# Four PSUM tiles of two banks, and one row maximum and one exponential for two heads

## The chip, the cores and the metric

The kernel runs on one core of a Trainium2 chip. The metric is the time of one execution on the device, in microseconds (us). The core has a matrix engine (TensorE, PE in the profile; its weight loads are listed apart as PEld), a vector engine (VectorE, DVE), a scalar engine (ScalarE, ACT), GpSimd (POOL) and a queue engine that issues most transfers (SyncE, SP). Matrix products land in PSUM, which has eight banks; one bank holds 512 fp32 numbers in each of 128 partitions. DVE and ACT read PSUM and so make its banks free again.

## The reference

Eight batches of 512 rows of 128 channels go through four layers. Each layer has an attention part and a feed-forward part, and each part is added to x after a layer norm: `x = x + layernorm(part(layernorm(x)))`. The two parts that the change edits directly are the softmax attentions of the first and of the fourth layer, with 16 heads of 8 channels:

```python
# layer 0 (and layer 3, there with a rotary embedding and a division by sqrt(8))
scores = jnp.einsum('hbqd,hbkd->hbqk', Q, K)
atten = jax.nn.softmax(scores, axis=-1)
out = jnp.einsum('hbqk,hbkd->hbqd', atten, V).reshape(b, s, -1)
```

Between them lie a gated mixer, a learned recurrence, a top-1 routed expert layer with a capacity, a linear attention and a top-k expert layer; after them four dense experts with weights for each row. All of it is fp32.

## The kernel before

It runs in three stages, told apart by what the engines do: stage I (about 0 to 740 us of the profiled execution) is the attention of layer 0, with the mixer, the recurrence and the routing as background work; stage II (about 740 to 1340 us) holds the rest of layers 0 and 1 and layer 2, many short chains taken in turns; stage III (about 1340 us to the end) is the attention of layer 3 with the dense experts as background work.

Instructions stand on each engine in the order in which the program writes them (`tc.manual_schedule()`); every engine works through its own list in order and waits at an instruction until the semaphores of that instruction allow it. The waits are put in by the framework, from the tiles that an instruction reads and writes.

**Attention.** A call is one batch with four heads; there are 32 calls in each attention. `Attention.run` goes through steps `g`, four steps (128 query rows each) to a call, so 128 steps in each attention. A step does two things for different calls. `score` takes the step `g + 7`: for each of four heads a product of queries with keys (tile `at_s`, L393), 128 rows by 512 columns in one bank, and on DVE the negated row maximum (`at_mx`, L394). `weigh` takes the step `g`: for each of four heads the transposed product (`at_st`, L400) with the row maximum already in it as an extra channel, and on ACT the exponential (`at_e`, L403). The four heads lie in four groups of 32 partitions (`32 * h`). A step writes these in the order score 0, weigh 2, score 1, weigh 3, then some background (`bg.between()`), then score 2, weigh 0, score 3, weigh 1, then the rest of the background (`bg.pull`). The four products of a half step thus use all four row groups of the matrix engine.

Once in four steps `maxima` turns the row maxima by a matrix transpose (`at_mx_ps`, L372), copies them on ACT (`at_mt`, L374) and sends them by four transfers on SP into the operand of `weigh`; `total_up` adds up the weighted values (`at_o`, 16 products, L411) with a copy on ACT (`at_ot`, L419); `finish` transposes that (`at_ops`, L425), and DVE divides (L428, L429).

**Background.** Generators that yield costs of PE and DVE. In stage III the largest is `L3Ffn.body`: `hidden` is one product (`l3f_h_ps`, L1923) with a relu on ACT (`l3f_hT`, L1924), `result` is four products (`l3f_y_ps`, L1930) with a weighted addition on DVE (`l3f_o`, L1933). `flip` (L239, copy on ACT L240) is a transpose of four blocks used everywhere.

**PSUM.** All eight banks are one ring: `bank()` hands out the next of eight tiles of one bank each. A new tile waits until the tile that had the bank eight requests earlier has been read. Scores and background draw from the same ring: a step takes eight banks for scores, and the background takes 1045 banks over the whole program.

Of the kernel before, what the change touches and what calls it, by code (L numbers as in the profile page):

```python
# [9 lines left out]
F32 = mybir.dt.float32  # L10
I32 = mybir.dt.int32
AF = mybir.ActivationFunctionType
ALU = mybir.AluOpType
AX = mybir.AxisListType
# [3 lines left out]
P = 128  # L18
# [3 lines left out]
NJ = S // P  # L22
# [48 lines left out]
class Ctx:  # L71


    def __init__(self, es: ExitStack, tc: tile.TileContext, consts: bass.AP):
        self.tc = tc
        nc = self.nc = tc.nc
        pool = lambda name, bufs, **kw: es.enter_context(tc.tile_pool(name=name, bufs=bufs, **kw))
        self.keep = pool("keep", 1)
        self.shared = pool("shared", 2)
        self.dram = pool("dram", 1, space=DRAM)  # L80

        self.c = self.keep.tile([P, C_ALL], F32, name="consts_sb", tag="consts_sb")
        nc.sync.dma_start(self.c, consts)
        self.ident = self.c[:, C_ID : C_ID + P]
        self.triu = self.c[:, C_TRIU : C_TRIU + P]
        self.ones = self.keep.tile([P, P], F32, name="ones", tag="ones")
        nc.vector.memset(self.ones, 1.0)
        self.mhalf = self.keep.tile([P, 8], F32, name="mhalf", tag="mhalf")
        nc.vector.memset(self.mhalf, -0.5)
        self.x = [self.keep.tile([P, NJ, D], F32, name=f"x{b}", tag=f"x{b}") for b in range(B)]  # L90

        self.home = self.keep

        self.ps = pool("ps", 1, space=PSUM)
        self.turn = [0]
        es.enter_context(tc.manual_schedule())

        self.brisk = False

    RING = 8  # L100

    @contextmanager
    def phase(self, name):
# [7 lines left out]
    def beside(self, name, side="left"):  # L111

        other = copy(self)
        with self.tc.tile_pool(name=name, bufs=2, side=side) as other.w:
            other.home = other.w
            yield other

    def bank(self, name):
        self.turn[0] += 1
        return self.ps.tile([P, 512], F32, name=name, tag=f"bank{self.turn[0] % self.RING}", bufs=1)  # L120

    def work(self, shape, name, bufs=2, dtype=F32):
        return self.w.tile(shape, dtype, name=name, tag=name, bufs=bufs)
# [197 lines left out]
class Attention:  # L321
# [58 lines left out]
    def run(self, n_calls, load, dst, done, scale, bg):  # L380


        cx, nc = self.cx, self.cx.nc
        total = NJ * n_calls
        mx, es, ots = {}, {}, {}

        def score(g, h):
            n, c = divmod(g, NJ)
            qk = self.qks[n % self.NQK][32 * h : 32 * h + 32]
            if n not in mx:  # L390
                mx[n] = cx.work([P, NJ, 4], "at_mx", bufs=3)
            s = cx.bank("at_s")
            nc.tensor.matmul(s, qk[:, 0, c * P : (c + 1) * P], qk[:, 1, :], start=True, stop=True)  # L393
            nc.vector.tensor_reduce(mx[n][:, c, h : h + 1], s, AX.X, ALU.max, negate=True)  # L394

        def weigh(g, h):
            n, c = divmod(g, NJ)
            qk = self.qks[n % self.NQK][32 * h : 32 * h + 32]
            s = cx.bank("at_st")
            nc.tensor.matmul(s, qk[:, 1, c * P : (c + 1) * P], qk[:, 0, :], start=True, stop=True)  # L400
            if g not in es:
                es[g] = cx.work([P, 4, S], "at_e", bufs=5)
            nc.scalar.activation(es[g][:, h, :], s, AF.Exp, scale=scale)  # L403

        def total_up(n):
            o = cx.bank("at_o")
            vp = self.pads[n % self.NPAD]
            for c in range(NJ):
                e = es.pop(NJ * n + c)
                for h in range(4):  # L410
                    nc.tensor.matmul(  # L411
                        o[32 * h : 32 * h + 32, :],
                        vp[:, c, h, :],
                        e[:, h, :],
                        start=(c == 0),
                        stop=(c == NJ - 1),
                    )
            ots[n] = cx.work([P, S], "at_ot")
            nc.scalar.copy(ots[n], o)  # L419

        def finish(n):
            ot = ots.pop(n)
            t = cx.bank("at_ops")
            for c in range(NJ):
                nc.tensor.transpose(t[:, c * P : (c + 1) * P], ot[:, c * P : (c + 1) * P], cx.ident)  # L425
            t = t.rearrange("p (c h d) -> p c h d", c=NJ, h=4)
            rec = cx.work([P, NJ, 4, 1], "at_rec")
            nc.vector.reciprocal(rec, t[:, :, :, 8:9])  # L428
            nc.vector.tensor_mul(dst(n), t[:, :, :, 0:8], rec.to_broadcast([P, NJ, 4, 8]))  # L429
            done(n)  # L430

        for g in range(-self.LEAD - self.LOAD, total + 2):
            ahead = g + self.LEAD
            is_s, is_t = 0 <= ahead < total, 0 <= g < total
            n, c = divmod(ahead + self.LOAD, NJ)
            if c == 0 and 0 <= n < n_calls:
                self.fill(n, *load(n))
            for i in (0, 2):

                for h in range(2):  # L440
                    if is_s:
                        score(ahead, i + h)
                    if is_t:
                        weigh(g, 2 - i + h)
                if i == 0 and (is_s or is_t):
                    bg.between()
            spent = 0.0
            n, c = divmod(ahead - 4, NJ)
            if c == 0 and 0 <= n < n_calls:
                self.maxima(n, mx.pop(n))  # L450
            n, c = divmod(g - NJ, NJ)
            if c == 0 and 0 <= n < n_calls:
                total_up(n)
                spent += 3.6
            if c == 1 and 0 <= n < n_calls:
                finish(n)
                spent += 0.5
            if is_s or is_t:
                bg.pull(spent)
# [147 lines left out]
class Mix:  # L607
# [16 lines left out]
    def load(self):  # L624
        cx, nc = self.cx, self.cx.nc
        W_r, W_k, W_v, mu_r, mu_k = self.args
        self.mu = cx.const([D, 2], "mu")
        nc.sync.dma_start(self.mu[:, 0:1], mu_r.rearrange("(d o) -> d o", o=1))
        nc.sync.dma_start(self.mu[:, 1:2], mu_k.rearrange("(d o) -> d o", o=1))
        raws = []  # L630
        for i, w in enumerate((W_r, W_k, W_v)):
            raws.append(cx.work([P, D], f"l0f_raw{i}", bufs=1))
            nc.sync.dma_start(raws[-1], w)
        self.nu = cx.const([D, 2], "nu")
        yield
        yield
        yield
        nc.vector.tensor_scalar(self.nu, self.mu, -1.0, 1.0, ALU.mult, ALU.add)
        t = cx.bank("l0f_w_ps")
        for i in range(3):  # L640
            nc.tensor.transpose(t[:, i * P : (i + 1) * P], raws[i], cx.ident)
        w = cx.const([P, 3, P], "w0f")
        nc.scalar.copy(w[:, 0:2, :].rearrange("p i d -> p (i d)"), t[:, : 2 * P])

        nc.scalar.mul(w[:, 2, :], t[:, 2 * P : 3 * P], 0.5)
        self.wr, self.wk, self.wv = (w[:, i, :] for i in range(3))
        yield 0.4
# [1414 lines left out]
```

## Time and profile before

| | |
|---|---|
| time, three runs | 2126.2, 2128.79 (median), 2131.81 us |
| the profiled execution | 2132.52 us; its span from first to last instruction 2130.7 us |
| granted PE clock, mean of the span | 0.871 |
| busy: PEld, ACT, POOL | 1012.4, 1085.9, 500.2 us |
| L393 MATMUL at_s | 2048 records, two for each product, mean 655 ns |
| L394 TENSOR_REDUCE at_mx | 1024, mean 681 ns |
| L403 ACTIVATE at_e | 1024, mean 597 ns |
| L419 COPY at_ot | 64, mean 585 ns |
| L374 COPY at_mt | 64, mean 238 ns |
| L1924 ACTIVATE l3f_hT | 128, mean 683 ns |
| L1933 SCALAR_TENSOR_TENSOR l3f_o | 128, mean 348 ns |

Busy time of a matrix product is modelled at its end, and products in different row groups overlap, so a busy PE is not a full PE. The duration of a DVE or ACT instruction is longer than the distance to the next one behind it, because the end of one overlaps the start of the next.

### The profile page before, as it was taken

The page shows a single profiled execution, that of the slowest core. Times are in us where ns is not written, and L with a number is a line of the kernel's source. Part 1 is how long each engine was busy: PE and PEld are TensorE (multiplying, and loading weights), DVE is VectorE, ACT ScalarE, POOL GpSimd, SP SyncE. Part 2 cuts the span into 40 slices and gives each one's busy share as a digit, 9 for nine tenths or more (in the row PEclk, how much of TensorE's full clock was granted, in tenths as well). Part 3 has the DMA queues.
Part 4 walks back from the last instruction along what each step waited for, and adds up shares of the span by engine and source line. Part 5 has one row for each costly group of instructions (what it writes and reads, how often), then busy time and mean ns, then how long its engine had stood idle before and what let it go on. Part 6 is the DMA issues. An engine that isn't in the chain of part 4 may idle for free.

```text
span 2130.7 us, 31833 instructions
## 1 busy us (share of the span) xinstructions
PE 1772.0 (83%) x10886; PEld 1012.4 (48%) x10886; DVE 1290.8 (61%) x4012; ACT 1085.9 (51%) x2272; POOL 500.2 (23%) x566
## 2 busy tenths in 40 slices
PE   3999999898989967649446773799999999999996
PEld 1444545454534456437335552444554454545454
DVE  2777786777777665546447422777666666665522
ACT  1566655555554732346552221366666565665653
POOL 1001111112121122442523485222212121110001
PEclk7999988899988887659565786799999999999998
DMA  5212101011100032016214132111101010100000
GB/s 127 39 33 39 34 16 38 14 39 22 32 16 15 14 104 83 23 27 180 79 50 124 24 42 36 31 32 29 27 9 31 11 27 12 29 12 6 9 6 10
DMA packets 198064, 81.83 MB, mean 38 GB/s; under 512 B 97604, under 2 KB 189674, under 8 KB 197904
## 3 DMA queue, kind: packets, MB, share of 16 engines
q1 hardware_dynamic: 190224, 73.61, 14.3%
q0 software_dynamic: 7680, 6.19, 1.9%
q8 instruction: 87, 1.43, 0.3%
q14 instruction: 73, 0.60, 0.1%
HBM read 45.25 MB, written 31.59 MB: 36 GB/s over the span
## 4 chain that ended last, share of the span: by engine, by line
PE 55%; DVE 23%; ACT 6%; issue 6%; POOL 5%; DMA 3%; SPq 2%; POOLq 0%; ACTq 0%; DVEq 0%
PE at_o L411 11%; PE at_s L393 11%; DVE at_mx L394 8%; PE at_st L400 6%; PE l3f_y_ps L1930 5%; PE l3f_h_ps L1923 5%; DVE ln_st L203 2%; PE flip L239 2%; POOL l2f_out L1686 2%; POOL ln_rs L194 1%; PE l1f_h_ps L1155 1%; PE l1f_y_ps L1177 1%; POOL l2f_xg L1081 1%; PE at_ops L425 1%; DVE ln_mv L205 1%
## 5 line engine op out<-in xcount | busy, mean ns | idle before, releaser
L394 DVE TENSOR_REDUCE at_mx<-at_s 128x1 f32<-128x512 f32 x1024 | 642.3, 681 | 302.3 <-PE at_st L400 233.9
L393 PE MATMUL at_s<-qk 32*128 32x512 f32 x2048 | 612.0, 655 | 35.6 <-DMA qk<-qk_zero 21.3
L403 ACT ACTIVATE at_e<-at_st 128x512 f32<-128x512 f32 x1024 | 535.7, 597 | 193.6 <-PE at_st L400 152.4
L400 PE MATMUL at_st<-qk 32*128 32x512 f32 x2048 | 610.2, 655 | 18.4 <-DVE at_mx L394 12.6
L194 POOL TENSOR_TENSOR ln_rs<-ln_ve,mhalf 128x4 f32<-128x4 f32 x136 | 138.3, 1017 | 837.5 <-DVE ln_ve L188 773.7
L393 PEld LDWEIGHTS at_s<-qk 32*128 32x128 f32 x2048 | 232.2, 194 | 177.4 <-issue 57.7
L400 PEld LDWEIGHTS at_st<-qk 32*128 32x128 f32 x2048 | 240.5, 192 | 111.7 <-issue 41.8
L411 PE MATMUL at_o<-at_e,pad_v 128*32 128x512 f32 x2048 | 254.2, 641 | 14.8 <-DVE at_mx L394 14.8
L411 PEld LDWEIGHTS at_o<-at_e,pad_v 128*32 128x32 f32 x2048 | 66.9, 117 | 197.5 <-issue 173.8
L1930 PEld LDWEIGHTS l3f_y_ps<-w3f,l3f_hT 128*128 128x128 f32 x1024 | 131.8, 197 | 46.3 <-issue 26.8
L1930 PE MATMUL l3f_y_ps<-w3f,l3f_hT 128*128 128x128 f32 x1024 | 136.9, 282 | 3.2 <-ACT l3f_hT L1924 2.0
L419 ACT COPY at_ot<-at_o 128x512 f32<-128x512 f32 x64 | 37.5, 585 | 199.5 <-PE at_o L411 199.5
L1923 PE MATMUL l3f_h_ps<-l3f_xT,w3f 128*128 128x512 f32 x256 | 131.2, 611 | 0.0
L1924 ACT ACTIVATE l3f_hT<-l3f_h_ps,w3f_b1c 128x512 f32<-128x512 f32 x128 | 85.0, 683 | 64.1 <-PE l3f_h_ps L1923 64.0
L1933 DVE SCALAR_TENSOR_TENSOR l3f_o<-l3f_y_ps,l3f_w,l3f_o 128x128 f32<-128x128 f32 x128 | 44.4, 348 | 93.3 <-PE l3f_y_ps L1930 93.1
L217 ACT ACTIVATE l_xn<-x,ln_off,ln_rs 128x128 f32<-128x128 f32 x96 | 39.5, 482 | 81.5 <-DVE ln_off L211 75.4
L239 PE MATMUL flip<-consts_sb,l_xn 128*128 128x128 f32 x96 | 29.6, 398 | 54.4 <-ACT l_xn L217 54.1
L203 DVE BATCH_NORM_STATS2 ln_st<-x 128x6 f32<-128x128 f32 x256 | 55.2, 278 | 18.2 <-POOL x L937 12.4
L1686 POOL DMA_INDIRECT l2f_out<-l2f_y,l2f_idx x32 | 50.5, 1579 | 21.9 <-DVE l2f_y L1683 13.1
L1923 PEld LDWEIGHTS l3f_h_ps<-l3f_xT,w3f 128*128 128x128 f32 x256 | 42.2, 194 | 23.9 <-issue 10.0
L1773 POOL TENSOR_TENSOR l_qk<-l_r,consts_sb 128x256 f32<-128x256 f32 x32 | 21.9, 686 | 133.2 <-DVE l_r L1768 133.2
L366 POOL COPY pad_v<-l_in 128x128 f32<-128x128 f32 x32 | 9.4, 294 | 185.4 <-DMA l_in<-l_v 147.9
(412 smaller groups left out, 2551.0 us busy)
## 6 DMA issues: line engine op xcount, KB each, us to landing
l1f_w<-in_L_ffn_w SPq DMA_DIRECT2D x32, 256.0 KB
l2f_parts<-l2f_out SPq DMA_DIRECT2D x32, 256.0 KB
l2f_out<-l1f_zero SPq DMA_DIRECT2D x24, 256.0 KB
l_qk<-l_qkT SPq DMA_DIRECT2D x16, 256.0 KB
qk<-l_qk SPq DMA_DIRECT2D x128, 32.0 KB
qk<-at_mt SPq DMA_DIRECT2D x256, 2.0 KB
qk<-l_qkT SPq DMA_DIRECT2D x128, 32.0 KB
l2f_x<-l2f_rows SPq DMA_DIRECT2D x8, 272.0 KB
```

Source lines behind the costliest of these rows:

```text
L194: self.nc.gpsimd.tensor_tensor(rs, ve, self.mhalf[:, :NJ], ALU.pow)
L203: nc.vector.bn_stats(st[:, j, :], src[:, j, :])
L239: self.nc.tensor.transpose(t[:, j * P : (j + 1) * P], src[:, j, :], self.ident)
L393: nc.tensor.matmul(s, qk[:, 0, c * P : (c + 1) * P], qk[:, 1, :], start=True, stop=True)
L394: nc.vector.tensor_reduce(mx[n][:, c, h : h + 1], s, AX.X, ALU.max, negate=True)
L400: nc.tensor.matmul(s, qk[:, 1, c * P : (c + 1) * P], qk[:, 0, :], start=True, stop=True)
L403: nc.scalar.activation(es[g][:, h, :], s, AF.Exp, scale=scale)
L411: nc.tensor.matmul(o[32 * h : 32 * h + 32, :], vp[:, c, h, :], e[:, h, :], start=(c == 0), stop=(c == NJ - 1),)
L1686: nc.gpsimd.indirect_dma_start(out=self.pairs.summed[s], out_offset=bass.IndirectOffsetOnAxis(ap=idx[e][:, s : s + 1], axis=0), in_=ys[e][ ...
L1923: nc.tensor.matmul(hp, self.w1[:, e, f * P : (f + 1) * P], xt, start=True, stop=True)
L1924: nc.scalar.activation(hts[e][:, f], hp, AF.Relu, bias=self.b1c[:, f, e : e + 1])
L1930: nc.tensor.matmul(yp[:, :D], hts[e][:, f, js], self.w2[:, e, f, :], start=(f == 0), stop=(f == NF - 1))
```

## The change

PSUM becomes a ring of four tiles of two banks. `twin()` hands out a whole tile; `bank()` hands out its first half and, at the next request, its second half; a `twin()` in between drops a half that is left over. A half step of attention now asks for one tile for two `weigh` products and one for two `score` products, writes the two transposed products, then the two products for the maxima, then one exponential over 2 x 512 columns and one reduction over 2 x 512 columns. Everything else that used a bank, so all of the background, `maxima`, `total_up` and `finish`, draws halves.

```diff
         self.turn = [0]
+        self.half = []
...
-    RING = 8
+    RING = 4
...
+    def twin(self, name):
+
+        self.half.clear()
+        self.turn[0] += 1
+        return self.ps.tile([P, 2, 512], F32, name=name, tag=f"twin{self.turn[0] % self.RING}", bufs=1)
+
     def bank(self, name):
-        self.turn[0] += 1
-        return self.ps.tile([P, 512], F32, name=name, tag=f"bank{self.turn[0] % self.RING}", bufs=1)
+
+        if self.half:
+            return self.half.pop()
+        t = self.twin(name)
+        self.half.append(t[:, 1, :])
+        return t[:, 0, :]
...
-        def score(g, h):
+        def products(s, g, i, side):
+
             n, c = divmod(g, NJ)
-            qk = self.qks[n % self.NQK][32 * h : 32 * h + 32]
+            for h in (i, i + 1):
+                qk = self.qks[n % self.NQK][32 * h : 32 * h + 32]
+                nc.tensor.matmul(
+                    s[:, h - i, :],
+                    qk[:, side, c * P : (c + 1) * P],
+                    qk[:, 1 - side, :],
+                    start=True,
+                    stop=True,
+                )
+
+        def score(g, i, s):
+            n, c = divmod(g, NJ)
             if n not in mx:
                 mx[n] = cx.work([P, NJ, 4], "at_mx", bufs=3)
-            s = cx.bank("at_s")
-            nc.tensor.matmul(s, qk[:, 0, c * P : (c + 1) * P], qk[:, 1, :], start=True, stop=True)
-            nc.vector.tensor_reduce(mx[n][:, c, h : h + 1], s, AX.X, ALU.max, negate=True)
-
-        def weigh(g, h):
-            n, c = divmod(g, NJ)
-            qk = self.qks[n % self.NQK][32 * h : 32 * h + 32]
-            s = cx.bank("at_st")
-            nc.tensor.matmul(s, qk[:, 1, c * P : (c + 1) * P], qk[:, 0, :], start=True, stop=True)
+            nc.vector.tensor_reduce(mx[n][:, c, i : i + 2], s, AX.X, ALU.max, negate=True)
+
+        def weigh(g, i, s):
             if g not in es:
                 es[g] = cx.work([P, 4, S], "at_e", bufs=5)
-            nc.scalar.activation(es[g][:, h, :], s, AF.Exp, scale=scale)
+            nc.scalar.activation(es[g][:, i : i + 2, :], s, AF.Exp, scale=scale)
...
-                for h in range(2):
-                    if is_s:
-                        score(ahead, i + h)
-                    if is_t:
-                        weigh(g, 2 - i + h)
+                if is_t:
+                    st = cx.twin("at_st")
+                    products(st, g, 2 - i, 1)
+                if is_s:
+                    s = cx.twin("at_s")
+                    products(s, ahead, i, 0)
+                if is_t:
+                    weigh(g, 2 - i, st)
+                if is_s:
+                    score(ahead, i, s)
                 if i == 0 and (is_s or is_t):
                     bg.between()
```

## The prediction

> **What bounds the kernel now.** I read first the page's busy times and its slices, then the costliest groups, then busy times by stretch, then the timeline of single steps.
>
> ```profile
> PE 1772.0 (83%) x10886; PEld 1012.4 (48%) x10886; DVE 1290.8 (61%) x4012; ACT 1085.9 (51%) x2272; POOL 500.2 (23%) x566
> ...
> PE   3999999898989967649446773799999999999996
> ...
> L394 DVE TENSOR_REDUCE at_mx<-at_s 128x1 f32<-128x512 f32 x1024 | 642.3, 681 | 302.3 <-PE at_st L400 233.9
> L403 ACT ACTIVATE at_e<-at_st 128x512 f32<-128x512 f32 x1024 | 535.7, 597 | 193.6 <-PE at_st L400 152.4
> L400 PE MATMUL at_st<-qk 32*128 32x512 f32 x2048 | 610.2, 655 | 18.4 <-DVE at_mx L394 12.6
> ```
>
> PE is nearly always busy in both attention stages (slices 2 to 14 and 27 to 39), and DVE and ACT mostly wait for PE: 302.3 us ahead of the maxima, 193.6 us ahead of the exponentials, against 18.4 us of PE ahead of L400. So PE sets the pace, and the next rows show how purely:
>
> ```profile
> 300.00:400.00 100.00, 93.20 (x569) 47.79 (x563) 74.92 (x218) 56.55 (x122) 15.79 (x19) 0.83 0.14 28
> 1100.00:1200.00 100.00, 61.41 (x261) 51.26 (x260) 61.06 (x287) 25.27 (x69) 36.31 (x50) 0.53 0.30 86
> 1500.00:1600.00 100.00, 96.31 (x660) 51.12 (x660) 67.71 (x176) 61.65 (x125) 19.36 (x24) 0.98 0.09 19
> ```
>
> (After the stretch: PE, PEld, DVE, ACT, POOL busy, then the granted PE clock.) In the timeline a step's eight score products take 1.93 us when nothing holds them (1553.09 to 1555.02). Adding up the blocks of score products in the trace gives 398 us in stage I and 318 us in stage III, against 128 x 1.93 = 247 us each. So stage I has 151 us and stage III only 71 us in which score products wait or run at half clock. In stage III PE is the limit; in stage I PE and DVE (75%) hold each other up; in stage II short chains do.
>
> **Part 1: one instruction for two heads.** A back-to-back run without background shows the price of single instructions:
>
> ```profile
> 132.49 6.99 ACT L403 ACTIVATE at_e<-at_st 128x512 f32<-128x512 f32 x12 [0.35 <-PE at_st L400]
> 132.76 7.25 DVE L394 TENSOR_REDUCE at_mx<-at_s 128x1 f32<-128x512 f32 x12
> ```
>
> That is 0.604 us for a reduction and 0.583 us for an exponential (four in 2.06 us, 0.515 each, where they don't wait). No row has a pair. Statistics on DVE take 691 ns for 512 columns (L565) and 278 for 128 (L203): 1.08 ns a column, so about 0.05 us of 0.604 is fixed. ACT copies take 585 ns for 512 columns and 474 for 384: 0.87 ns a column, leaving 0.07 of 0.515. With 512 pairs each, 26 us of DVE and 36 us of ACT go away, at most 62 us if both were on the path, and nothing where PE is. The reader may also start later, but four products run side by side and both heads are ready together (products from 1559.40, first reduction at 1560.56). So start is no loss, but release is coarser: a tile is refilled only when both heads are read, 1.16 us of products after a pair of about 1.16 + 0.08 us. The round is 2.40 us, and the single heads needed 4 x 0.604 = 2.42 us a step: the saving on DVE is spent again even where DVE was the limit. I put part 1 at -25 us (bounds -62 and 0).
>
> The Trainium skill has a rule against this part. "Perfetto Trace Analysis", section "Optimizing Scalar/DVE Operations", has larger operations help where the engine is saturated, and smaller ones where it is not but makes others wait. Here DVE is 61% and ACT 51% busy, the second case; by the rule part 1 would gain nothing, and the sum below would end 25 us higher.
>
> **Part 2: the order of the products.** Score, weigh, score, weigh becomes weigh, weigh, score, score. Heads 2, 3 and 0, 1 still fill all four row groups, so 1.93 us stays. A weigh that waits now holds both score products behind it on PE; that is within the bounds of part 1.
>
> **Part 3: two banks under one tile.** This decides. The waits that the framework put into the changed program are known before it runs. Of the 1045 banks that are not scores, 453 are second halves; 448 of them have a first product that waits on its own semaphore for the instruction that *reads the first half*, though the banks differ. Before, these products had a bank of their own and waited only for a reading eight banks back. PE works in order, so everything behind stands still too: the next scores, and for those DVE and ACT. One step of stage III shows it:
>
> ```profile
> 1555.02 0.28 PE L372 MATMUL at_mx_ps<-consts_sb,at_mx 128*16 128x128 f32 x1
> 1555.14 0.60 PE L425 MATMUL at_ops<-consts_sb,at_ot 128*128 128x128 f32 x4
> 1555.60 0.66 PE L239 MATMUL flip<-consts_sb,l3f_xn 128*128 128x128 f32 x4
> 1556.09 1.02 PE L1923 MATMUL l3f_h_ps<-l3f_xT,w3f 128*128 128x512 f32 x2
> 1556.28 0.24 ACT L374 COPY at_mt<-at_mx_ps 16x128 f32<-16x128 f32 x1
> 1556.42 0.57 ACT L240 COPY l3f_xT<-flip 128x512 f32<-128x512 f32 x1
> 1557.45 1.16 PE L1930 MATMUL l3f_y_ps<-w3f,l3f_hT 128*128 128x128 f32 x8 [0.34 <-DVE at_mx L394]
> 1558.45 1.02 PE L1923 MATMUL l3f_h_ps<-l3f_xT,w3f 128*128 128x512 f32 x2
> 1558.65 0.35 DVE L1933 SCALAR_TENSOR_TENSOR l3f_o<-l3f_y_ps,l3f_w,l3f_o 128x128 f32<-128x128 f32 x1 [0.16 <-PE l3f_y_ps L1930]
> ```
>
> at_ops starts 0.12 us after at_mx_ps. As its second half it must wait for the copy at_mt, which stands behind exponentials and ends at 1556.52: 1.38 us late. The product h after flip would wait for the copy that ends at 1556.99, 0.90 us late; the product h after y for the addition that ends at 1559.00, 0.55 us late.
>
> I took this lateness for every pair in the trace of before: end of the last reader of the first half, plus 0.05 us (from a reader's end to a waiting product: an exponential ends at about 304.39, weights load at 304.43), minus the start of the second half's first product. 424 pairs could be matched by name:
>
> - stage I: 82 pairs, 112 us. Of these, at_ops behind at_mx_ps is 30 pairs at 1.93 us = 58 us.
> - stage II: 153 pairs, 166 us.
> - stage III: 189 pairs, 262 us. at_ops behind at_mx_ps 30 x 1.95 = 59, y behind h 25 x 2.20 = 55, h behind y 39 x 0.97 = 38, h behind h 11 x 1.90 = 21, the other 84 together 89.
>
> The 29 left I price at stage II's mean, 1.08 us: 32 us. All of it would be 112 + 166 + 262 + 32 = 572 us.
>
> It won't all be paid. A late reader is partly late because DVE and ACT have a backlog, and they work it off while PE waits. In stage III what remains is the reader itself: at_ops about 1.35 (the last exponential pair, about 1.0, plus 0.24 and two handovers), y behind h 0.9 (relu 0.69 and handovers), h behind y 0.6, others about 0.9. That is 41 + 23 + 23 + 10 + 76 = 173 us, 66%; I take 0.7, 183 us, since the 71 us of slack there are small. In stage I, DVE and ACT lose their feed after such a stop (in the step at 130 us, PE would resume 0.9 us later and DVE run dry), but scores that already waited for DVE hide a part: 0.6, 67 us. In stage II other chains wait anyway while PE does: 0.5 of 198, 99 us. Bounds: 0.3, 0.25 and 0.5 give 34 + 50 + 131 = 215 us; the full lateness gives 572.
>
> **Part 4: the clock of PE.** It follows PE's load in the rows above: 0.98 at 96% busy, 0.83 at 93% and 0.53 at 61%. With 183 us of stops stage III falls below 80% busy. If the clock there went from 0.98 to 0.88, some 650 us of PE work would take 72 us more, and in stage I 0.90 to 0.85 would add 33 us; half of it hides under the stops. With some 8 us in stage II I take 60 us; bounds 0 and 150.
>
> "TensorE: Matmul & The Clock Gate", section "What's actually happening", has the clock halve after an idle window of about 3.4 us. The stops here are shorter, so by the letter of that rule part 4 would be 0 and the sum 60 us lower; but the clock was 0.83 between 300 and 400 us with no gap on PE over 2.1 us. The row decides.
>
> **The sum.** 67 + 99 + 183 + 60 - 25 = 384 us. The span of 2130.7 us becomes 2515, the profiled run's 2132.5 us 2517; on the median 2128.8 it is 2513 us. The bounds added up: 215 + 0 - 62 = +153 us and 572 + 150 - 0 = +722 us. Both ends at once are unlikely; I go from 2290 to 2720.
>
> **Rivals.**
> - *The stops hide under waits that exist already.* For it: DVE and ACT wait a lot, and stage I has 151 us of slack. Against it: in stage III 71 us of slack stand against 262 us of lateness. With the low bounds 2129 + 153 to 165 = about 2285 us, chance 0.11.
> - *The clock goes down for good.* For it: 0.53 at 61% load. Full lateness and a stage III at 0.75 give 2129 + 572 + 100 = 2800 us, chance 0.12.
> - *Faster: the second half's reader is done in time.* If PE reached a second half only after the reader of the first, part 3 is nothing and part 1 counts: 2129 - 25 to - 62, about 2090 us. It decides once mean lateness falls below 25 / 453 = 0.06 us, against 540 / 424 = 1.27 us in the trace. Chance 0.03.
> - *The waits bite only in a few places and cancel with part 1*: within 0.3% (6 us, about what a measurement of this kernel can tell), 0.01.
>
> The forecast itself has 0.73: in all 0.96 slower, 0.01 same, 0.03 faster.
>
> **What would show it.** In the profile after: at_mx and at_e 512 times, at about 1.2 and 1.05 us each; at_ops beginning after the end of the copy at_mt in nearly every call; PE idle ahead of at_ops, l3f_h_ps and l3f_y_ps with ACT and DVE as releasers, some 300 us more idle PE; more half-clock time in stage III. It is wrong if stage III takes less than 100 us more, if PE does not wait before second halves, or if most of the loss stands ahead of score products.

## The result, and the profile after

The kernel after takes 2634.58 us (median of six runs, 2623.7 to 2638.7); the kernel before, run beside it on the same chip, takes 2129.82 us (median of six, 2123.37 to 2133.85). The ratio is 1.2369, with an interval of 1.2339 to 1.2399: 505 us slower, where the prediction had 384. The execution profiled took 2633.47 us, with a span of 2631.7 us and a mean granted PE clock of 0.843 against 0.871.

First the page's busy times, PE's slices, the slices of PE's granted clock, and the groups that answer to those shown of before:

```profile
PE 1897.4 (72%) x10886; PEld 1019.1 (39%) x10886; DVE 1264.0 (48%) x3500; ACT 1069.9 (41%) x1760; POOL 500.6 (19%) x566
...
PE   4888878778787666565556747877777777777776
...
PEclk9899988897988675586555866999899999999998
...
L415 DVE TENSOR_REDUCE at_mx<-at_s 128x2 f32<-128x1024 f32 x512 | 611.1, 1219 | 423.4 <-PE at_s L403 417.0
L420 ACT ACTIVATE at_e<-at_st 128x1024 f32<-128x1024 f32 x512 | 505.0, 1019 | 328.0 <-PE at_s L403 264.0
L403 PE MATMUL at_st<-qk 32*128 32x512 f32 x2048 | 578.0, 682 | 28.5 <-DVE at_mx L415 15.4
L442 PE MATMUL at_mx_ps<-consts_sb,at_ot 128*128 128x128 f32 x240 | 43.0, 306 | 89.4 <-ACT at_mt L385 89.4
```

The granted clock of the kernel before, in 40 slices of its own span, was this:

```profile
PEclk7999988899988887659565786799999999999998
```

PE was at 9 in most slices of the attention stages and is now at 7 or 8. DVE and ACT did their part of the change: 512 reductions and 512 exponentials of two heads each, 27 and 16 us less busy. Nothing else has become the limit, because DVE and ACT wait longer for PE than before (423.4 and 328.0 us ahead of these two groups, against 302.3 and 193.6). PE itself stands still. The last row names the largest single place: the transposes of `finish`, called `at_ops` before. A second half carries the name of the tile that it lies in, so here they are called `at_mx_ps`, with `finish`'s line L442. PE stood for 89.4 us ahead of them, all of it for the copy `at_mt`, which reads the other half. In the kernel before PE's waits ahead of `at_ops` were these two, 9.8 us, and none was for `at_mt`:

```profile
PE at_ops L425 <- ACT at_e L403: 8.4, 7, 2.1
PE at_ops L425 <- ACT at_ot L419: 1.4, 2, 0.7
```

PE's waits of the kernel after (releaser, us in all, times, longest) list the same thing for other pairs. L1945 is the product of `hidden` and L1952 that of `result`:

```profile
PE at_mx_ps L442 <- ACT at_mt L385: 89.4, 60, 4.2
PE l3f_y_ps L1945 <- DVE l3f_o L1955: 31.0, 39, 2.0
PE l3f_h_ps L1952 <- ACT l3f_hT L1946: 30.2, 25, 2.5
...
PE at_st L403 <- DVE at_mx L415: 15.4, 13, 2.2
```

Each of the first three lines is a product that waits for the instruction that reads the other bank of its tile. The fourth, a score product that waits for a reduction, is small and was 12.6 us before.

One stretch of the timeline in stage III, 18 us long, lets this be watched (start, length, engine and line; in brackets the idle time ahead and what ended it):

```profile
1904.90 1.02 ACT L420 ACTIVATE at_e<-at_st 128x1024 f32<-128x1024 f32 x1
1905.05 0.91 PE L1788 MATMUL l_qkv_ps<-w3a,xnT 128*128 128x384 f32 x2 [0.31 <-ACT at_e L420]
1906.58 0.28 DVE L1791 TENSOR_TENSOR l_v<-l_qkv_ps,w3a_b 128x128 f32<-128x128 f32 x1
1906.91 1.13 PE L1945 MATMUL l_qkv_ps<-l3f_xT,w3f 128*128 128x512 f32 x2 [0.95 <-DVE l_v L1791]
...
1914.93 0.59 ACT L436 COPY at_ot<-at_o 128x512 f32<-128x512 f32 x1 [2.58 <-PE at_o L428]
1915.57 0.91 PE L1788 MATMUL at_o<-w3a,xnT 128*128 128x384 f32 x2 [0.70 <-ACT at_ot L436]
...
1919.47 0.24 ACT L385 COPY at_mt<-at_mx_ps 16x128 f32<-16x128 f32 x1
1919.76 0.66 PE L442 MATMUL at_mx_ps<-consts_sb,at_ot 128*128 128x128 f32 x4 [0.76 <-ACT at_mt L385]
```

Three times a product starts 0.05 us after another engine has finished with the *other* half: 1906.58 + 0.28 = 1906.86 and the product at 1906.91; 1914.93 + 0.59 = 1915.52 and 1915.57; 1919.47 + 0.24 = 1919.71 and 1919.76. PE lost 0.95, 0.70 and 0.76 us there. The releaser named in the brackets is that reader each time.

Where the time lies, by stage. Stage I ends with the last `at_st` of the first attention, stage III begins with the first `at_s` of the second. PE's idle time is where no product ran; "lost to half clock" is half of the time in which a product ran while the granted clock was 0.5. The clock records of the traces hold two values alone, 1 and 0.5; a fall is a stretch at 0.5. Differences are taken before rounding.

| | stage I | stage II | stage III |
|---|---|---|---|
| length before, after, us | 743, 848 (+105) | 595, 738 (+143) | 792, 1045 (+253) |
| PE idle before, after, us | 89, 192 (+103) | 218, 293 (+76) | 52, 249 (+197) |
| lost to half clock before, after, us | 59, 86 (+27) | 100, 153 (+52) | 22, 51 (+29) |
| mean granted clock before, after | 0.904, 0.887 | 0.704, 0.652 | 0.965, 0.943 |
| falls to half clock before, after | 22, 36 | 23, 24 | 8, 21 |
| mean length of a fall before, after, us | 6.5, 5.3 | 15.6, 21.6 | 6.4, 5.6 |

One more sum over the traces goes to the cause: PE's idle time right ahead of the first products of the 453 second halves (before, the same products, in a bank of their own) went from 124 to 504 us, +380: 83 of it in stage I, 118 in stage II and 179 in stage III. With the 108 us of the clock (27 + 52 + 29) that is 488 of 505.

### The profile page after: what moved, and what is told of

The parts are those of the page before. It is cut to its first block, busy times and chain, and to the rows that moved or that the text cites. A ratio compares the mean times of both kernels' runs of the same rounds, so it can differ in the third digit from the quotient of the medians.

```text
span 2631.7 us, 30977 instructions
## 1 busy us (share of the span) xinstructions
PE 1897.4 (72%) x10886; PEld 1019.1 (39%) x10886; DVE 1264.0 (48%) x3500; ACT 1069.9 (41%) x1760; POOL 500.6 (19%) x566
## 4 chain that ended last, share of the span: by engine, by line
PE 52%; DVE 21%; ACT 16%; issue 5%; POOL 3%; DMA 2%; SPq 1%; ACTq 0%; POOLq 0%; DVEq 0%
PE at_st L403 9%; PE at_o L428 8%; DVE at_mx L415 7%; ACT at_e L420 6%; PE at_s L403 4%; PE l3f_y_ps L1952 3%; PE l3f_h_ps L1945 2%; DVE ln_st L214 2%; PE l3f_y_ps L1945 2%; PE at_mx_ps L442 1%; PE l1f_h_ps L1177 1%; PE l3f_h_ps L1952 1%; ACT l3f_hT L1946 1%; PE l2f_h_ps L1687 1%; ACT at_ot L436 1%
## 5 line engine op out<-in xcount | busy, mean ns | idle before, releaser
L415 DVE TENSOR_REDUCE at_mx<-at_s 128x2 f32<-128x1024 f32 x512 | 611.1, 1219 | 423.4 <-PE at_s L403 417.0
L420 ACT ACTIVATE at_e<-at_st 128x1024 f32<-128x1024 f32 x512 | 505.0, 1019 | 328.0 <-PE at_s L403 264.0
L403 PE MATMUL at_s<-qk 32*128 32x512 f32 x2048 | 577.1, 696 | 24.1 <-DMA qk<-qk_zero 21.1
L403 PEld LDWEIGHTS at_st<-qk 32*128 32x128 f32 x2048 | 190.2, 203 | 194.0 <-issue 82.7
L403 PEld LDWEIGHTS at_s<-qk 32*128 32x128 f32 x2048 | 186.5, 205 | 108.0 <-issue 54.5
L1952 PEld LDWEIGHTS l3f_y_ps<-w3f,l3f_hT 128*128 128x128 f32 x712 | 97.0, 204 | 37.8 <-issue 23.9
L442 PE MATMUL at_mx_ps<-consts_sb,at_ot 128*128 128x128 f32 x240 | 43.0, 306 | 89.4 <-ACT at_mt L385 89.4
L1952 PE MATMUL l3f_y_ps<-w3f,l3f_hT 128*128 128x128 f32 x712 | 101.6, 290 | 5.9 <-DVE l3f_o L1955 4.0
L1945 PE MATMUL l3f_h_ps<-l3f_xT,w3f 128*128 128x512 f32 x130 | 79.6, 709 | 12.2 <-ACT l3f_hT L1946 9.8
L1946 ACT ACTIVATE l3f_hT<-l3f_h_ps,w3f_b1c 128x512 f32<-128x512 f32 x65 | 44.5, 685 | 79.3 <-PE l3f_h_ps L1945 79.3
L1945 PE MATMUL l3f_y_ps<-l3f_xT,w3f 128*128 128x512 f32 x78 | 44.0, 646 | 31.0 <-DVE l3f_o L1955 31.0
L442 PEld LDWEIGHTS at_mx_ps<-consts_sb,at_ot 128*128 128x128 f32 x240 | 27.3, 150 | 100.9 <-ACT at_mt L385 100.9
```

Source lines behind the costliest of these rows:

```text
L403: nc.tensor.matmul(s[:, h - i, :], qk[:, side, c * P : (c + 1) * P], qk[:, 1 - side, :], start=True, stop=True,)
L415: nc.vector.tensor_reduce(mx[n][:, c, i : i + 2], s, AX.X, ALU.max, negate=True)
L420: nc.scalar.activation(es[g][:, i : i + 2, :], s, AF.Exp, scale=scale)
L1945: nc.tensor.matmul(hp, self.w1[:, e, f * P : (f + 1) * P], xt, start=True, stop=True)
L1946: nc.scalar.activation(hts[e][:, f], hp, AF.Relu, bias=self.b1c[:, f, e : e + 1])
L1952: nc.tensor.matmul(yp[:, :D], hts[e][:, f, js], self.w2[:, e, f, :], start=(f == 0), stop=(f == NF - 1))
```

## The experiments

Three theories stood against each other. A: the framework makes the second half's products wait for the reader of the first half. R: a ring of four coarse tiles is what hurts, whoever waits for whom inside a tile. P: the pair instructions and the order of the products hurt. All times are medians; ratios are to the kernel before on the same chip, with 95% intervals.

**Banks apart.** The kernel after, with the waits between different halves of a tile taken out wherever the two instructions share nothing else. The halves are different banks, and a bank is still waited for.

```diff
+def apart(tc, twins):
...
+    for name, us in uses.items():
+        if name.startswith(("at_s_", "at_st_")):
+            continue
+        for k, (late, h) in enumerate(us):
+            for early, g in us[:k]:
+                if h != g and late.engine != early.engine and not shares(late, early, name):
+                    tc.declare_no_dep(late, early, reason="other bank")
```

> The changed kernel with the same four tiles, order and pair instructions, but the framework is told that an access to one bank of a tile does not depend on an access to the other bank, unless the two also share another tile. The second halves' waits for the first half's reader are gone (448 before, 22 left where a real value is handed on). Theory A (the tied halves are the loss): 2090 to 2180 us, PE idle ahead of at_ops and of the expert products back to about what it was. Rival R (a ring of four coarse tiles is the loss): still over 2450 us. Rival P (pair instructions or the order of products are the loss): still over 2450 us.

2163.91 us, ratio 1.017 (1.0129 to 1.021). Of the 505 us, 471 are gone. The page shows PE back at 8 and 9 in the attention stages, with the same pair instructions:

```profile
PE 1742.7 (81%) x10886; PEld 973.5 (45%) x10886; DVE 1260.8 (58%) x3500; ACT 1059.8 (49%) x1760; POOL 500.3 (23%) x566
...
PE   3898988898888868658447783898989899999996
...
L418 DVE TENSOR_REDUCE at_mx<-at_s 128x2 f32<-128x1024 f32 x512 | 611.4, 1218 | 349.9 <-PE at_s L406 343.8
```

PE's idle time ahead of the second halves is 116 us, less than before the change. So A holds, and R and P together come to 34 us net in this form.

**The waits alone.** The kernel before, with eight tiles of one bank and single heads, and only the waits added: the first product of what would be a second half waits for the last readers of what would be its first half.

```diff
+        if name in ("at_s", "at_st"):
+            self.half.clear()
+        elif self.half:
+            self.pairs.append((self.half.pop(), t.tensor.name))
+        else:
+            self.half.append(t.tensor.name)
...
+    for first, second in pairs:
+        for r in {r.engine: r for r in reads[first]}.values():
+            tc.add_manual_dep(writes[second][0], r.name, info, reason="first half read")
```

> The kernel before with eight single banks, one head to an instruction and the old order; the only addition is that the second of each two background banks, paired as the changed kernel pairs them, waits with its first product for the last readers of the first. Theory A: 2560 to 2690 us, all of the loss without any of the change's other parts. Rivals R and P: 2130 to 2200 us.

2660.88 us, ratio 1.2507 (1.2469 to 1.2545). The whole loss appears with nothing of the change but its waits. It is even 26 us more than after; the kernel after has the pair instructions on top, and the next experiment prices them. PE's waits of this kernel name the same products and releasers:

```profile
PE at_ops L434 <- ACT at_mt L383: 118.3, 60, 4.3
PE l3f_h_ps L1932 <- DVE l3f_o L1942: 33.9, 39, 2.2
PE l3f_y_ps L1939 <- ACT l3f_hT L1933: 32.9, 25, 3.0
```

**One head at a time.** The kernel after, with each pair instruction split into two.

```diff
-            nc.vector.tensor_reduce(mx[n][:, c, i : i + 2], s, AX.X, ALU.max, negate=True)
+            for h in range(2):
+                nc.vector.tensor_reduce(mx[n][:, c, i + h : i + h + 1], s[:, h, :], AX.X, ALU.max, negate=True)
...
-            nc.scalar.activation(es[g][:, i : i + 2, :], s, AF.Exp, scale=scale)
+            for h in range(2):
+                nc.scalar.activation(es[g][:, i + h, :], s[:, h, :], AF.Exp, scale=scale)
```

> The changed kernel with its tiles and order, but each pair instruction split into two for one head each. Theory A: 2635 to 2680 us, as slow as the changed kernel or a little slower, since at most 62 us of DVE and ACT work come back. Rival P (the long instructions delay what waits for them): 2130 to 2450 us.

2689.34 us, ratio 1.2637 (1.2591 to 1.2682): 55 us more than after, and 9 us above the window of theory A, which had allowed at most 45 us for the split. The pair instructions are no part of the loss; they save. (Against the waits alone this kernel has the new order and the coarse ring too, and is 28 us slower.)

**A whole tile for every request.** The kernel after, without second halves, so that nothing can be tied; each single request uses up a tile of two banks.

```diff
         t = self.twin(name)
-        self.half.append(t[:, 1, :])
         return t[:, 0, :]
```

> The changed kernel, but bank() takes a whole new tile each time and leaves its second half unused: no tied halves, and 2069 tiles through the ring in place of 1616. Theory A: well below the changed kernel, 2200 to 2450 us, the rest being the shorter ring. Rival R (the coarse ring is the loss): above 2635 us, since the ring is used up faster still.

2239.35 us, ratio 1.0527 (1.0494 to 1.056). Throwing away every second bank of the background, which makes 2069 tiles out of 1616, costs far less than using it under the framework's waits.

**The order alone.** The kernel before, with the two transposed products and their exponentials ahead of the two others.

```diff
                 for h in range(2):
-                    if is_s:
-                        score(ahead, i + h)
                     if is_t:
                         weigh(g, 2 - i + h)
+                for h in range(2):
+                    if is_s:
+                        score(ahead, i + h)
```

> The kernel before with eight single banks and single-head instructions; only the order within a half step is new: weigh, weigh, score, score. With the banks kept apart the changed kernel was 34 us over the kernel before, though the sum had it 25 us under. If the order makes these 34 us: 2160 to 2190 us. If it is neutral, as the sum had it: 2115 to 2145 us.

2131.47 us, ratio 1.0009 (0.999 to 1.0029): no change.

**Banks apart, one head at a time.** The edits of the first and the third experiment together; their diffs are above.

> The changed kernel with the banks kept apart (2164 us) and each pair instruction split into two. If the pair instructions save and the coarse ring of four tiles costs: slower than 2164, 2185 to 2225 us. If the pair instructions themselves are what costs 34 us (a longer reader ahead of whatever takes its tile next): 2120 to 2150 us.

2189.61 us, ratio 1.0273 (1.0238 to 1.0308). Against banks apart with pairs (2163.91) the pairs save 26 us here (22 by the two ratios). What is left of the change in this kernel is the ring of four tiles and the order, and it costs some 60 us against the kernel before (0.0273 x 2128 = 58). The order is worth nothing in the ring of eight, so the 58 us are put down to the coarse ring, as this kernel asks for its tiles.

**Banks apart, order of before.** The first experiment with the products interleaved as before, and with the tile for the maxima asked for first.

```diff
+                if is_s:
+                    s = cx.twin("at_s")
                 if is_t:
                     st = cx.twin("at_st")
-                    products(st, g, 2 - i, 1)
-                if is_s:
-                    s = cx.twin("at_s")
-                    products(s, ahead, i, 0)
+                for k in range(2):
+                    if is_s:
+                        product(s, ahead, i, 0, k)
+                    if is_t:
+                        product(st, g, 2 - i, 1, k)
```

> The changed kernel with the banks kept apart and the four products of a half step in the old order: score, weigh, score, weigh, into two tiles. If the order makes the 34 us: 2120 to 2140 us. If the coarse ring does: 2150 to 2180 us.

2205.0 us, ratio 1.0358 (1.0323 to 1.0393). A miss: neither window holds it, and it changed two things at once. The last two experiments take them apart.

**A single kind of wait.** The second experiment with only the 60 waits of `at_ops` for the copy `at_mt`.

```diff
     for first, second in pairs:
+        if not first.startswith("at_mx_ps"):
+            continue
         for r in {r.engine: r for r in reads[first]}.values():
```

> The kernel before with only 60 of the 453 waits added: at_ops waits for the copy of at_mx_ps. The lateness of these 60 pairs in the trace of before adds up to 117 us. If each stop is paid by itself, nearly in full, as the idle time ahead of at_ops in the kernel with all waits says (118 us): 2220 to 2270 us. By the factors of the prediction (0.6 to 0.7, no clock): about 2205 us. If stops hurt only in mass, through the clock: under 2170 us.

2239.82 us, ratio 1.0519 (1.0491 to 1.0546): +112 us, 1.87 us for each wait. The lateness that the prediction had read for these pairs was 58 + 59 = 117 us, so it was paid nearly whole. The 112 us hold a loss of clock too: PE's idle time grew by 102 us in all, and the loss to half clock by 32. PE stands ahead of these products:

```profile
PE at_ops L434 <- ACT at_mt L383: 116.9, 60, 4.3
```

**Leftover halves kept.** Of the coarse ring's price it was open whether it comes from the halves that are dropped when the scores ask for a tile. Here they are kept until the ring comes round.

```diff
     def twin(self, name):
-
-        self.half.clear()
...
         if self.half:
-            return self.half.pop()
+            at, second = self.half.pop()
+            if self.turn[0] - at < self.RING:
+                return second
         t = self.twin(name)
-        self.half.append(t[:, 1, :])
+        self.half.append((self.turn[0], t[:, 1, :]))
```

> As e1_banks_apart (2163.91 us), but a second half that is left over when the scores ask for a tile is kept for the next single request instead of being dropped, unless the ring has come round. Open is why e1 and e6_apart_one_head stand some 35 and 60 us above the kernel before. Theory D (the dropped halves make the ring short): 2125 to 2145 us, and PE's waits for exponentials ahead of at_mx_ps, at_o and flip, some 72 us together in e1, fall by half or more. Theory C (a tile of two banks comes free only when both heads are read, whatever the singles do): 2150 to 2175 us, with the same waits as in e1.

2160.8 us, ratio 1.017 (1.0147 to 1.0193), the same as banks apart; PE's waits for `at_e` come to 99 us in all against 96 there. The dropped halves cost nothing.

**The order of the tiles, and the order of the products.** Banks apart with one of the two changes each: first only the tile for the maxima asked for ahead of the other, as shown, then only the interleaved products, as in the diff of banks apart, order of before.

```diff
+                if is_s:
+                    s = cx.twin("at_s")
                 if is_t:
                     st = cx.twin("at_st")
                     products(st, g, 2 - i, 1)
                 if is_s:
-                    s = cx.twin("at_s")
                     products(s, ahead, i, 0)
```

> As e1_banks_apart, products in the same order (two transposed ones first), but the tile for the maxima is asked for ahead of the tile for the exponentials. e7_apart_old_order changed this and the order of the products together and took 2205.0 us, 41 more than e1. Theory T (the order of the tiles counts: the first single bank after a half step then comes back from a reduction of about 1.2 us in place of an exponential of about 1.0 us): 2195 to 2215 us, PE's waits ahead of at_mx_ps and at_o are for at_mx. Theory O (the order of the products counts): 2155 to 2175 us.

> As e1_banks_apart, tiles asked for in the same order, but the products interleaved as in the kernel before (maxima, transposed, maxima, transposed). Theory T: 2155 to 2175 us. Theory O: 2195 to 2215 us, since each of the two tiles is complete only after the last pair of products.

2205.39 us, ratio 1.0389 (1.0346 to 1.0432), for the tiles; 2171.48 us, ratio 1.0234 (1.0201 to 1.0267), for the products. So it is the order in which tiles are asked for. That the tile asked for first is also the one filled last is not the reason: banks apart, order of before (2205.0 us, ratio 1.0358) and the second kernel here (2171.48, 1.0234) fill both tiles side by side and differ in the order of asking alone. PE's waits, of banks apart and then with the tile for the maxima first, show what it changes:

```profile
PE at_mx_ps L386 <- ACT at_e L423: 24.8, 49, 2.7
PE at_st L406 <- ACT at_e L423: 21.6, 18, 2.0
PE at_o L431 <- ACT at_e L423: 10.7, 28, 0.9
```

```profile
PE at_st L406 <- DVE at_mx L418: 45.7, 39, 3.9
PE at_mx_ps L386 <- DVE at_mx L418: 34.2, 60, 1.3
PE at_o L431 <- DVE at_mx L418: 28.2, 45, 1.5
```

The same products wait, but for the reduction in place of the exponential. The first background tile after a step takes over the tile that the step asked for first; it comes free when both heads in it are read. The reduction takes 1.22 us and the exponential 1.02, and the waits for either come to 114 us in banks apart (96 for `at_e`, 18 for `at_mx`) and to 179 us with the other order (24 and 155). In the kernel before they were 59 us (15 and 44), and with banks apart and one head at a time 129 (106 and 24). So the coarse ring adds 55 to 70 us of such waits, about its price of 58.

## Why the prediction was right, and where it was off

**Part 3 was the cause, and right in size.** The prediction summed the lateness of the first halves' readers, took part of it, and got 349 us of stops; PE's idle time ahead of second halves grew by 380. By stage it planned 67, 99 and 183 us. Ahead of the second halves PE's idle time grew by 83, 118 and 179: 0.74, 0.60 and 0.68 of the lateness, where 0.6, 0.5 and 0.7 had been taken. PE's whole idle time grew by 103, 76 and 197, so in stage II some 42 us of the new stops only took the place of old ones, as the prediction argued. The weak step is the backlog that ACT and DVE were to work off while PE stands, so that of `at_ops` only 1.35 of 1.95 us would remain. With these 60 waits alone there was no such relief: PE stood 116.9 us ahead of `at_ops`, 1.95 each, and with all waits 118.3. In the kernel after it is 89.4, 1.49 each, but there the `at_mx_ps` ahead of it waits 24.9 us for exponentials. For h behind y 31.0 of 39 x 0.97 = 38 us were paid, and for y behind h 30.2 of 55, where the prediction kept 23 us for either.

**Part 4 was mis-sized, and put in the wrong place.** The sum had 60 us for the clock; the loss to half clock grew by 108 us. The prediction expected stage III to fall from 0.98 to 0.88 when it is less than 80% busy. It fell from 0.965 to 0.943 over the whole stage. These are the three stretches of the kernel after that answer to those shown of before (PE, PEld, DVE, ACT, POOL busy, then the granted clock):

```profile
300.00:400.00 100.00, 78.61 (x472) 35.37 (x471) 62.40 (x175) 47.41 (x77) 17.71 (x20) 0.82 0.12 25
1100.00:1200.00 100.00, 62.16 (x288) 46.80 (x288) 36.64 (x161) 36.51 (x78) 19.24 (x18) 0.76 0.32 94
2000.00:2100.00 100.00, 74.58 (x463) 35.99 (x463) 46.77 (x101) 44.11 (x65) 16.83 (x21) 0.95 0.08 19
```

A clock of 0.95 stands beside 75% busy, and 0.76 beside 62%, where before there were 0.83 beside 93% and 0.53 beside 61%. So a busy share over 100 us does not give the clock, and the prediction's reading of three rows as a rule was wrong. Nearly half of the loss came where it planned least: stage II lost 52 us more to half clock, against some 8 planned, and stage III 29, against 36 (half of 72).

The traces show a rule on a shorter scale. In their clock records the value changes only in steps of 3.41 us. Cut at these steps, the kernel before, the kernel after and the waits alone agree. At full clock, all 95 windows with a product running for less than 40% of the time were followed by one at half clock, and of those with at least 80% only 17 of 808. At half clock, none of the 296 windows under 79% was followed by one at full clock, and of those with at least 90%, 178 of 227. In between it goes either way. This tells the stages apart: in the kernel after 14 of stage III's 305 windows are under 40% busy, 49 of stage II's 216. Stage II does not fall more often than before (24 times against 23), but it comes back later (21.6 us against 15.6): windows of at least 80% went from 78 of 175 to 65 of 216 there.

The Trainium skill ("TensorE: Matmul & The Clock Gate", section "What's actually happening") has the clock halve after an idle window of about 3.4 us, and by its letter part 4 would have been near 0, as most stops last 0.5 to 2 us. The length of the window agrees with the 3.41 us of the traces, but it need not be idle: of the 222 falls in those three traces 9 followed a window without any product. The time lost to half clock rose from 182 to 290 us in the kernel after and to 311 with the waits alone, and stayed at 182 with only the order changed.

**Part 1 had the wrong sign.** The step said -25 us, with bounds of -62 and 0, for the pair instructions and their coarser release together. All of the change without its tied halves cost +34 us (banks apart). The pair instructions did save what was expected of them alone (at most 62 us): 26 us with banks apart and 55 us with the halves tied. What the sum left out is the release. The prediction worked it out for the scores (a round of 2.40 us against 2.42) and found the saving spent again; it did not ask who draws the same tiles next. That is the background, which now waits until both heads of a tile are read, where it waited for a single head before: some 60 us.

The Trainium skill ("Perfetto Trace Analysis", section "Optimizing Scalar/DVE Operations") was weighed against this part: it has larger operations help if the engine is saturated. Here they help without that: DVE is 58% busy with banks apart and 48% busy in the kernel after, and the pairs still save 26 and 55 us there.

**Part 2 was right.** The order was put at nothing and is worth nothing (ratio 1.0009) in the ring of eight. In the coarse ring the order of products is worth some 8 us (14 by the ratios), but the order of *tiles*, which the prediction did not treat as a step, is worth 41 (47 by the ratios).

**The signs named.** 512 reductions at 1.219 us and 512 exponentials at 1.019 us, against about 1.2 and 1.05. `at_ops` starts after the copy `at_mt` in all 60 calls. PE's idle time grew by 376 us, against some 300. More half-clock time in stage III: yes, but less than thought. What would have refuted it did not come: stage III took 253 us more, not less than 100, and the blocks of score products, each up to the product behind it, grew from 398 to 405 us in stage I and from 318 to 339 in stage III, 28 us of 505.

**The sum.** 349 + 60 - 25 = 384 was short by 121 us: 31 from the stops, 48 from the clock, and 42 from the rest of the change, which the sum had at -25 and which is +17 when 380 and 108 are taken from 505. Measured alone, with banks apart, it is +34; the sums over the traces don't add up more closely than that. The rival in which the clock goes down for good (2800 us, 165 too much) fell, since stage III kept 0.943 where it needed 0.75. That the stops hide (2285 us) fell with PE's 380 us.

**What stays open.** Pair instructions over two banks that are each freed on their own, in a ring of eight, were not tried. By these runs they would keep the saving without the ring's price and without the ties; whether that beats the kernel before isn't shown. None of the versions here does.

## What to carry to other kernels

A wait is placed by what the framework takes for one object: before two buffers are put under one tile, ask which writer of the one now waits for which reader of the other, and read off the old trace how late that reader ends. Where the waiting engine sets the pace and works in order, count that lateness nearly whole, the loss of its clock included: here 112 of 117 us for 60 waits alone, and 531 of 572 for all of them. When instructions are merged and their buffers with them, the price is paid by whoever draws that buffer next; here it was lower by 41 us when the tile with the quicker reader was asked for first.

## What had not been expected

- 60 waits, each for an instruction that reads a bank which the waiting product does not touch, cost 112 us of 2128 (1.87 us each).
- PE's clock has two values and is set anew every 3.41 us: half after every full-clock window with less than 40% busy (95 of 95 in three traces), and back only after one with at least 79%. So stops of 0.5 to 2 us cost clock, and most where windows seldom get full again: stage II lost 52 us more, with 76 us more idle time, stage III 29 with 197.
- Two reductions of 1024 columns, back to back, take 2.36 us where four of 512 took 2.48 us, and two exponentials take 1.94 us where four took 2.06 (most frequent values in the two traces). For each instruction that is left out that is 0.06 us on either engine ((2.48 - 2.36) / 2 and (2.06 - 1.94) / 2), and the kernel gains 26 to 55 us from it.
- Which of two tiles of one half step is asked for first is worth 41 us, 2%, with every product and every reading unchanged.
